# A free place between the first exponentials of one head group, in a two-layer graph network kernel

## The chip, the cores and the metric

The kernel runs on one core of one Trainium2 chip. The metric is the device time of one execution in microseconds; the time of a kernel is the median over its runs. Five engines work in parallel[...]: TensorE (PE, with its weight loads shown as PEld), VectorE (DVE), ScalarE (ACT), GpSimd (POOL) and SyncE (SP), which here only issues transfers.

## The reference

Input `x` holds 128 graphs of 64 nodes with 768 features, `adj` a 64 x 64 adjacency for each graph. Two layers follow each other, both with a residual and a layer norm:

```python
# layer 0: similarity attention, three linear maps of h
u = einsum('bld,bmd->blm', h, h) / sqrt(d)
delta = softmax(u) * adjacency
attn = delta / (delta.sum(2) + 1e-10)
ctx = attn_left @ (h W_left + b) + diag(attn) * (h W_self + b) + attn_right @ (h W_right + b)
x = layernorm(x + relu(layernorm(ctx) * gamma + beta))
# layer 1: 12 heads of 64, masked softmax attention within each graph
q, k, v = split_heads(x @ Wq + bq), split_heads(x @ Wk + bk), split_heads(x @ Wv + bv)
scores = where(adj > 0, q k^T / sqrt(64) + 0.1 * adj, -9e15)
x = layernorm(x + softmax(scores) @ v)
```

Everything is fp32.

## The kernel before

The 8192 tokens are cut into 16 blocks (`NBLK`) of 512 tokens (eight graphs, four tiles of 128). The main loop runs over the blocks `n`. One pass of it interleaves the first layer of block `n + 1` with the second layer of block `n`, in this order on PE: the left and right products of block `n + 1` (`both_sides`, a nested seven-product scheme, from the fourth block on; two plain `side_part` calls before), its self product (`self_part`), the values of block `n` (`values`), and then the queries and keys of block `n` in three stages (`projected`, for head groups `hg` 0, 1 and 2, of four heads each). The last pass has no first layer; it begins with PE transposes (`transposed1`) and does the values last.

Each large product is done by a Strassen-like scheme of seven smaller products in place of eight. `seven` runs over them in the order `ORDER = (1, 2, 6, 5, 7, 4, 3)`, and for each over `j` = 0, 1. In `projected`, `j` = 0 is the queries and `j` = 1 the keys. That gives 14 places in a stage, each with three matmuls of 256 columns. Products 1, 6, 7 and 4 of one `j` accumulate one after the other on one PSUM bank (`ps_X`), products 2, and then 5 and 3, on another (`ps_Y`). Between them the partial sums are read out. This reading out is called eviction here. In `projected`, ACT evicts products 1, 6 and 7 to `uqk` with the bias (L801) and product 4 to `q` or `k` (L807); DVE adds `uqk` to products 2, 5 + 7 and 3 (L809). A matmul that accumulates on a bank can only run when the eviction of what the bank held is done: 4 needs the eviction of 7, and 7 that of 6. In `both_sides` (`nested`, `sub`) the inner products have the same dependences, with the order 6, 5, 7, then 1 and 2 of the next outer product, then 4 and 3; ACT's share of their evictions is the copy at L441.

Attention of a head group is done behind its projection. `scores(n, hg)` for head group 0 is called at place 2 of the stage of head group 1, for head group 1 at place 2 of the stage of head group 2, and for head group 2 in the next pass. It runs the 64 small score matmuls (L833), scales them on DVE (L837), and puts the rest into the queue `urgent`, as items: add the mask (L860), reduce to the maximum (L861), subtract it (L862), four steps of exponentials, a gap, and two transpositions on DVE (turn 0 and turn 1, L857). One step of exponentials is four ACT instructions of 32 rows by 256 elements (L853) and belongs to 32 partitions. `weighted` later multiplies with the values (L882), and its DVE evictions with the division (L892) go into the queue `first`.

After each place, `step` takes at most one item from each of three queues, `first`, `urgent` and `lazy`, in that order. The kind of an item says whether it may go now. An item of DVE work (no kind) goes only when no other such item has gone in this step. An `act` item goes only when ACT is free by plan: `seven`, called by `projected`, forbids it after two places. A `gap` goes always, and fills its place with nothing. In `sub`, `step` takes only from `first` and `urgent` behind inner products 5, 1 and 4, and no DVE item there. `settle` empties a queue up to the named items; `scores` calls it for all attention items that are left. After a first part that sets up the weights, the schedule is manual: on every engine the instructions run in the order in which they were written out.

In block 0 the weights of the first layer are also made ready for the nested scheme (`deepened`): three items at the head of `urgent`, from place 9 on of the head group 2 stage. In the lazy queue are, among others, the last normalizations of the first layer (L720). `finish` ends a block with sums and squares on ACT (L938, L941), a root, and stores.

The line that keeps ACT free after the places of the second half of 5 and the first half of 7:

```python
step(not taps_by_act or (i, j) not in ((5, 1), (7, 0)))
```

Of the kernel before, what the change touches and what calls it, by code (L numbers as in the profile page):

```python
# [17 lines left out]
P = 128  # L18
# [8 lines left out]
Q = 32  # L27
# [24 lines left out]
def gnn_two_layers(ctx: ExitStack, tc, x, adj, wl, bl, ws, bs, wr, br, gamma, beta,  # L52
# [68 lines left out]
    def later(key, *fs, queue=lazy):  # L121
        queue.extend((key, f) if callable(f) else (key, *f) for f in fs)

    def act(f):
        return f, "act"
# [7 lines left out]
    GAP = (gap, "gap")  # L133
# [24 lines left out]
    def freed():  # L158

        while first:  # L160
            first.popleft()[1]()

    def settle(key):

        for queue in (first, urgent, lazy):
            while any(item[0] == key or item[0][0] == key for item in queue):
                queue.popleft()[1]()
# [646 lines left out]
    def scores(n, hg, at_once=1, pool=None, gaps=1):  # L814

        blk = blocks[n]
        q, k = blk["qk"]  # L820
        settle("e")
        settle(("m", n))
        freed()

        s = l1s_p.tile([P, T * 4 * L], F32, tag="s", name="s").rearrange("p (t c r m) -> p t c r m", t=T, c=2, r=2)
        sc = [ps_mm.tile([P, T, 2, L], F32, tag="mm", name=f"sc{r}") for r in range(2)]
        for t in range(T):
            for c in range(2):
                for r in range(2):
                    rows = slice(r * HD, (r + 1) * HD)  # L830
                    for g in range(2):
                        tok = slice(t * P + g * L, t * P + (g + 1) * L)
                        nc.tensor.matmul(sc[r][g * L : (g + 1) * L, t, c, :], lhsT=q[rows, c, tok],  # L833
                                         rhs=k[rows, c, tok], start=True, stop=True)
        m8, add = blk["m8"], blk["add"]
        for r in range(2):
            nc.vector.tensor_tensor(s[:, :, :, r, :], sc[r], m8[:, :, None, :].to_broadcast([P, T, 2, L]), ALU.mult)  # L837
        s4 = s.rearrange("p t c r m -> p t (c r) m")
        s8 = s.rearrange("p t c r m -> p (t c r) m")
        pairs = s.rearrange("p t c r m -> p (t c) (r m)")  # L840
        mx = st.tile([P, T * 4], F32, tag="mx1", name="mx1")

        def exponentials(groups):
            if 0 in groups:
                blk["eT", hg] = (pool or l1e_p).tile([P, T, 2, P], F32, tag="lr" if pool else "eT", name="eT")
            e = blk["eT", hg].rearrange("p t c i -> p (t c) i")
            for a in groups:
                rows = slice(a * Q, (a + 1) * Q)
                for b in range(P // Q):
                    cols = slice(b * Q, (b + 1) * Q)  # L850
                    to = (b, a) if n < NBLK - 1 else (a // 2 * 2 + b % 2, b // 2 * 2 + a % 2)
                    to = [slice(k * Q, (k + 1) * Q) for k in to]
                    nc.scalar.activation(e[to[0], :, to[1]], pairs[rows, :, cols], AF.Exp)  # L853

        def turn(h):
            e = blk["eT", hg][:, h * 2 : h * 2 + 2].rearrange("p t c i -> p (t c i)")
            nc.vector.transpose(e, e)  # L857

        later(("e", n, hg),
              lambda: nc.vector.tensor_tensor(s4, s4, add[:, :, None, :].to_broadcast([P, T, 4, L]), ALU.add),  # L860
              lambda: nc.vector.tensor_reduce(mx, s8, AX.X, ALU.max),  # L861
              lambda: nc.vector.tensor_tensor(s8, s8, mx[:, :, None].to_broadcast([P, T * 4, L]), ALU.subtract),  # L862
              *[act(partial(exponentials, range(a, a + at_once))) for a in range(0, P // Q, at_once)], *[GAP] * gaps,
              *([partial(turn, 0), partial(turn, 1)] if pool is None else [lambda: (turn(0), turn(1))]), queue=urgent)

    def weighted(n, hg):
# [153 lines left out]
    for n in range(NBLK):  # L1020
# [20 lines left out]
        if p >= 0:  # L1041
            one = left if not last else qk[0]
            at(one, 2, scores, p, 2, *((1,) if last else (2, None, 4)))
            at(one, 5, weighted, p, 1)
            if not last and m < DEEP:
                at(left, 13, weighted, p, 2)
                at(right, 0, finish, p)
            elif not last:
                at(right, 1, weighted, p, 2)
                at(right, 2, finish, p)  # L1050
            else:
                at(qk[1], 5, weighted, p, 2)
# [84 lines left out]
        else:  # L1137
            transposed1(n)
            at(qk[0], 9, lambda: later(("m", n), *mask(n), queue=urgent))
            blocks[n]["S"] = combined(blocks[n]["xT"])  # L1140
            combined4(blocks[n]["S"])
        at(qk[1], 2, scores, n, 0)
        at(qk[2], 2, scores, n, 1)
        if not last:
            at(qk[2], 5, weighted, n, 0)
# [136 lines left out]
```

## Time and profile before

| What | us |
|---|---|
| Median of 3 runs (2923.8 to 2925.47) | 2923.98 |
| The profiled execution's own time | 2923.8 |
| Its span in the trace | 2922.1 |
| PE busy (98% of the span) | 2872.4 |
| PE weight loads busy (66%) | 1931.7 |
| DVE busy (68%) | 1979.6 |
| ACT busy (38%) | 1120.4 |
| POOL busy (25%) | 732.2 |
| ACT exponentials, L853, 768 of 414 ns | 317.8 |
| ACT evictions of queries and keys, L801, 288 of 471 to 473 ns | 136.0 |
| PE waits for these evictions (16 times) | 9.5 |

Lines such as L801 are lines of the kernel. A row of a timeline gives the start in us from the span's start, the duration, the engine, the line, the operation with output and input tiles and shapes, the number of instructions merged into the row, and in brackets how long the engine sat idle before and what released it. One fp32 matmul appears as two records, so that a place of a projection stage, three matmuls, has six. Matmuls are pipelined: one starts before the end that is shown for the one before it, and that end is modelled. The granted clock of TensorE was 0.998 of full speed.

### The profile page before, as it was taken

The page shows a single profiled execution, that of the slowest core. Times are in us where ns is not written, and L with a number is a line of the kernel's source. Part 1 is how long each engine was busy: PE and PEld are TensorE (multiplying, and loading weights), DVE is VectorE, ACT ScalarE, POOL GpSimd, SP SyncE. Part 2 cuts the span into 40 slices and gives each one's busy share as a digit, 9 for nine tenths or more (in the row PEclk, how much of TensorE's full clock was granted, in tenths as well). Part 3 has the DMA queues.
Part 4 walks back from the last instruction along what each step waited for, and adds up shares of the span by engine and source line. Part 5 has one row for each costly group of instructions (what it writes and reads, how often), then busy time and mean ns, then how long its engine had stood idle before and what let it go on. Part 6 is the DMA issues. An engine that isn't in the chain of part 4 may idle for free.

```text
span 2922.1 us, 49871 instructions
## 1 busy us (share of the span) xinstructions
PE 2872.4 (98%) x17578; PEld 1931.7 (66%) x17578; DVE 1979.6 (68%) x3973; ACT 1120.4 (38%) x2107; POOL 732.2 (25%) x879
## 2 busy tenths in 40 slices
PE   9999999999999999999999999999999999999997
PEld 5658566585665857657576675766757567585685
DVE  6778777676676766757667576766767667676655
ACT  0005224354243443434444334343434424354255
POOL 3133123213042140412405123051230512314110
PEclk9999999999999999999999999999999999999999
DMA  9788877859577595875958669486694956849443
GB/s 340 231 272 272 251 214 202 243 143 286 153 207 238 160 274 149 226 220 167 270 145 246 195 181 267 137 269 174 184 260 138 285 160 195 246 139 288 140 127 100
DMA packets 440662, 613.18 MB, mean 210 GB/s; under 512 B 53584, under 2 KB 416720, under 8 KB 440416
## 3 DMA queue, kind: packets, MB, share of 16 engines
q1 hardware_dynamic: 362960, 495.93, 56.5%
q10 hardware_dynamic: 60848, 44.05, 8.0%
q0 software_dynamic: 16608, 70.01, 6.6%
q8 instruction: 143, 2.34, 0.3%
q14 instruction: 103, 0.84, 0.1%
HBM read 539.43 MB, written 77.27 MB: 211 GB/s over the span
## 4 chain that ended last, share of the span: by engine, by line
PE 93%; ACT 3%; POOL 2%; DVE 1%; issue 1%; DMA 0%; POOLq 0%; SPq 0%; ACTq 0%
PE ps_X L389 36%; PE ps_Y L389 27%; PE ps_Y L643 11%; PE ps_X L643 10%; PE ps_ctx L682 3%; ACT eT L853 2%; PE sc L833 2%; PE ps_y L882 2%; PE u L532 2%; POOL q L342 1%; ACT L853 1%; ACT uqk L801 1%; PE ps_x L291 0%; POOL q L341 0%; POOL q L343 0%
## 5 line engine op out<-in xcount | busy, mean ns | idle before, releaser
L389 PE MATMUL ps_X<-xT,wqk 128*128 128x256 f32 x1728 | 395.8, 381 | 9.5 <-ACT uqk L801 9.5
L853 ACT ACTIVATE eT<-s 32x256 f32<-32x256 f32 x768 | 317.8, 414 | 172.4 <-DVE s L862 162.4
L389 PEld LDWEIGHTS ps_X<-xT,wqk 128*128 128x128 f32 x1728 | 325.8, 190 | 67.0 <-ACT uqk L801 16.2
L322 POOL TENSOR_TENSOR S<-hT 128x768 f32<-128x768 f32 x16 | 28.9, 1807 | 1132.7 <-PE ps_Y L389 1102.1
L389 PE MATMUL ps_Y<-S,wqk 128*128 128x256 f32 x1152 | 264.3, 379 | 0.0
L687 ACT ACTIVATE unused<-o 128x768 f32<-128x768 f32 x60 | 50.6, 844 | 499.6 <-DVE o L684 346.1
L389 PEld LDWEIGHTS ps_Y<-S,wqk 128*128 128x128 f32 x1152 | 218.9, 190 | 29.8
L443 DVE TENSOR_TENSOR lr<-ps_Y,u_deep 128x384 f32<-128x384 f32 x273 | 152.1, 557 | 109.1 <-PE ps_Y L643 83.4
L643 PE MATMUL ps_Y<-wlr,q 128*128 128x384 f32 x546 | 208.5, 491 | 0.0
L389 PE MATMUL ps_X<-wv,xT 128*128 128x384 f32 x576 | 195.5, 489 | 0.0
L801 ACT ACTIVATE uqk<-ps_X,bq 128x256 f32<-128x256 f32 x144 | 68.1, 473 | 325.0 <-PE ps_X L389 323.9
L809 DVE TENSOR_TENSOR q<-ps_Y,uqk 128x256 f32<-128x256 f32 x144 | 61.0, 424 | 177.5 <-ACT uqk L801 89.3
L389 PE MATMUL ps_X<-ws,hT 128*128 128x384 f32 x540 | 179.2, 486 | 0.0
L643 PE MATMUL ps_X<-wlr,q 128*128 128x384 f32 x364 | 151.0, 497 | 14.6 <-POOL q L342 6.0
L389 PEld LDWEIGHTS ps_X<-wv,xT 128*128 128x128 f32 x576 | 108.0, 190 | 80.4 <-issue 8.4
L892 DVE SCALAR_TENSOR_TENSOR o<-ps_y,rz,o 128x64 f32<-128x64 f32 x720 | 154.7, 278 | 6.4
L443 DVE TENSOR_TENSOR u_deep<-ps_X,lr 128x384 f32<-128x384 f32 x195 | 107.5, 551 | 68.2 <-PE ps_X L643 66.6
L389 PEld LDWEIGHTS ps_X<-ws,hT 128*128 128x128 f32 x540 | 102.5, 190 | 71.4
L643 PEld LDWEIGHTS ps_Y<-wlr,q 128*128 128x128 f32 x546 | 101.6, 190 | 67.2
L420 DVE TENSOR_TENSOR u<-ps_X,bv 128x384 f32<-128x384 f32 x96 | 53.4, 557 | 132.5 <-PE ps_X L389 132.5
L389 PE MATMUL ps_X<-S,wqk 128*128 128x256 f32 x576 | 138.2, 385 | 0.0
L389 PE MATMUL ps_Y<-xT,wqk 128*128 128x256 f32 x576 | 135.6, 385 | 0.0
(258 smaller groups left out, 5471.6 us busy)
## 6 DMA issues: line engine op xcount, KB each, us to landing
wlr<-lr_d SPq DMA_DIRECT2D x819, 192.0 KB, 3.5
wqk<-qk_d SPq DMA_DIRECT2D x672, 192.0 KB, 2.4
wv<-d_v SPq DMA_DIRECT2D x192, 192.0 KB, 2.7
ws<-d_s SPq DMA_DIRECT2D x180, 192.0 KB, 5.8
wv<-in_L_gnn_Wv_dram SPq DMA_DIRECT2D x144, 192.0 KB, 4.1
ws<-in_L_gnn_W_self_dram SPq DMA_DIRECT2D x135, 192.0 KB, 5.4
xa<-in_x_dram SPq DMA_DIRECT2D x64, 384.0 KB, 5.3
sq<-in_x_dram ACTq DMA_DIRECT2D x56, 384.0 KB, 7.7
```

Source lines behind the costliest of these rows:

```text
L389: nc.tensor.matmul(ps, lhsT=a, rhs=b, start=(c == 0 and i in (1, 2, 5)), stop=(c == len(fs) - 1), skip_group_check=True)
L420: recent["u"] = evicted[nm] = nc.vector.tensor_tensor(u, ps, bias[nm][:, b * HALF : (b + 1) * HALF], ALU.add)
L443: nc.vector.tensor_tensor(dst, view(ps), add, ALU.add)
L532: nc.tensor.matmul(u[g * L : (g + 1) * L, t, :], lhsT=xT[:, c, tok], rhs=xT[:, c, tok], start=(c == 0), stop=(c == KC - 1))
L643: nc.tensor.matmul(ps, lhsT=a, rhs=b, start=(k == 0 and j in (1, 2, 5)), stop=(k == len(fs) - 1), skip_group_check=True)
L682: nc.tensor.matmul(ps[g * L : (g + 1) * L, 0:HALF], lhsT=blk["aT"][:, t, g * L : (g + 1) * L], rhs=blk["lr"][t][:, g, cols], start=True, s ...
L801: nc.scalar.activation(u, ps, AF.Identity, bias=bias["qk"[j]][:, c : c + 1])
L809: nc.vector.tensor_tensor(dst, ps, part, ALU.add)
L833: nc.tensor.matmul(sc[r][g * L : (g + 1) * L, t, c, :], lhsT=q[rows, c, tok], rhs=k[rows, c, tok], start=True, stop=True)
L853: nc.scalar.activation(e[to[0], :, to[1]], pairs[rows, :, cols], AF.Exp)
L882: nc.tensor.matmul(y[r, h][cols, t, c, :], lhsT=eT[rows, 2 * h + t, c, cols], rhs=v[rows, 2 * h + t, g, hg + c * HC, :], start=True, stop= ...
L892: nc.vector.scalar_tensor_tensor(res[:, r, c, hg, :], ps[:, t, c, 0:HD], rz[:, t, c : c + 1], res[:, r, c, hg, :], ALU.mult, ALU.add)
```

## The change

The list of items that `scores` puts into `urgent` gets one `GAP` more, for head group 1 alone (`hg == 1`) and in all 16 blocks: behind the first of the four steps of exponentials. The other head groups keep their list. Nothing else is edited.

```diff
               lambda: nc.vector.tensor_reduce(mx, s8, AX.X, ALU.max),
               lambda: nc.vector.tensor_tensor(s8, s8, mx[:, :, None].to_broadcast([P, T * 4, L]), ALU.subtract),
-              *[act(partial(exponentials, range(a, a + at_once))) for a in range(0, P // Q, at_once)], *[GAP] * gaps,
+              *(part for a in range(0, P // Q, at_once) for part in
+                (act(partial(exponentials, range(a, a + at_once))), *([GAP] if hg == 1 and a == 0 else []))),
+              *[GAP] * gaps,
               *([partial(turn, 0), partial(turn, 1)] if pool is None else [lambda: (turn(0), turn(1))]), queue=urgent)
```

## The prediction

> **What bounds the kernel now.** I began with the page's busy times and its chain that ended last, since they say which engine sets the end.
>
> ```profile
> PE 2872.4 (98%) x17578; PEld 1931.7 (66%) x17578; DVE 1979.6 (68%) x3973; ACT 1120.4 (38%) x2107; POOL 732.2 (25%) x879
> ...
> PE 93%; ACT 3%; POOL 2%; DVE 1%; issue 1%; DMA 0%; POOLq 0%; SPq 0%; ACTq 0%
> ```
>
> TensorE (PE) carries 93% of the chain. From one projection stage to the same one a block later it takes 179.75 us, over and over. So a change is worth the time by which it moves PE's starts, and nothing else. The list of waits, PE's alone, says where PE stands for ScalarE (ACT):
>
> ```profile
> PE ps_X L389 <- ACT uqk L801: 9.5, 16, 0.6
> ```
>
> Sixteen waits of 0.59 us. I went through PE's timeline for all 16. Fifteen lie at one place, in the projection of head group 2 in blocks 0 to 14 (284.44, 468.38, 648.13, ... 2802.55 us). The sixteenth, at 2780.98, is in head group 1 of block 14. Block 15 has none. This is ACT's timeline, then PE's, in block 4 (start, duration, engine, line, operation, idle before):
>
> ```profile
> 1001.87 0.47 ACT L801 ACTIVATE uqk<-ps_X,bk 128x256 f32<-128x256 f32 x1 [2.11 <-PE ps_X L389]
> 1002.36 1.28 ACT L853 ACT_TABLE_LOAD   x1
> 1003.66 3.40 ACT L853 ACTIVATE eT<-s 32x256 f32<-32x256 f32 x8
> 1007.08 0.47 ACT L801 ACTIVATE uqk<-ps_X,bq 128x256 f32<-128x256 f32 x1
> 1007.46 0.47 ACT L801 ACTIVATE uqk<-ps_X,bk 128x256 f32<-128x256 f32 x1
> 1007.95 1.69 ACT L853 ACTIVATE eT<-s 32x256 f32<-32x256 f32 x4
> 1009.66 0.47 ACT L807 ACTIVATE q<-ps_X,bq 128x256 f32<-128x256 f32 x1
> 1010.16 1.69 ACT L853 ACTIVATE eT<-s 32x256 f32<-32x256 f32 x4
> 1011.87 0.47 ACT L807 ACTIVATE k<-ps_X,bk 128x256 f32<-128x256 f32 x1
> 1013.74 0.48 ACT L441 COPY u_deep<-ps_X 128x384 f32<-128x384 f32 x1 [1.39 <-PE ps_X L643]
> ```
>
> ```profile
> 983.34 5.34 PE L389 MATMUL ps_X<-xT,wqk 128*128 128x256 f32 x24
> 988.52 2.75 PE L389 MATMUL ps_Y<-S,wqk 128*128 128x256 f32 x12
> ...
> 1004.26 2.75 PE L389 MATMUL ps_X<-xT,wqk 128*128 128x256 f32 x12
> 1007.61 2.86 PE L389 MATMUL ps_X<-xT,wqk 128*128 128x256 f32 x12 [0.59 <-ACT uqk L801]
> 1010.30 2.75 PE L389 MATMUL ps_Y<-S,wqk 128*128 128x256 f32 x12
> 1012.89 0.81 PE L643 MATMUL ps_X<-wlr,hT 128*128 128x384 f32 x2
> 1013.54 1.45 PE L643 MATMUL ps_Y<-wlr,hT 128*128 128x384 f32 x4
> 1014.83 0.81 PE L643 MATMUL ps_X<-wlr,q 128*128 128x384 f32 x2
> ```
>
> I write (7,0) for product 7 of the queries, (7,1) of the keys. (7,·) starts at 1004.26, (4,·) at 1007.61, (3,·) at 1010.30. The eight exponentials in one piece (3.40 us) are the first two steps; the eviction of (7,0) stands behind them until 1007.08, and (4,0), which accumulates on the same bank, waits for it. One stage earlier (first two lines) the same two products run without a stop: 988.52 - 983.34 = 5.18 us. Here they take 1010.30 - 1004.26 = 6.04. **The wait therefore costs 0.86 us**, more than the 0.59 shown, because modelled ends overlap the next start[...].
>
> [...] (7,0) was ready at about 1005.82 and was evicted at 1007.08. [...] so I reckon in starts. [...] here the load is 1.28 us and the exponential follows after 0.02[...]. [...] in the trace they lead by 0.2 to 0.3 us, but at 1007.61 weight load and matmul start together, so the wait holds both.
>
> **The change part by part.** No instruction is added or removed. One empty item enters the queue behind step 0 of the exponentials. Step 0 still leaves behind (6,1). The item uses up the place behind (5,0), where step 1 went. Behind (5,1) and (7,0) no ACT item may go, so step 1 follows the eviction of (7,1), step 2 that of (4,0), step 3 that of (4,1); the gap falls behind (3,0), the first transposition (turn 0, L857) behind (3,1), turn 1 into the next stage, behind its (7,2), since behind its first product no VectorE (DVE) item is taken.
>
> *Saved.* Step 0 ends at 1003.66 + 1.69 = 1005.35. In a stage that isn't held, evictions start 1.56 and 2.85 us after (7,·) starts (block 15: products at 2864.10, evictions at 2865.66 and 2866.95). So (7,0) is evicted 1005.82 to 1006.29 and (7,1) 1007.11 to 1007.58, both before (4,0) at 1006.85 and (4,1) at 1008.15 need them. Saved: 0.86.
>
> *Given back.* ACT now idles 0.47 us before the first eviction and 0.82 before the second, and pays it at the end. With the spacings of the trace (eviction to exponentials 0.49 to 0.50, exponentials to what follows 1.71): step 1 at 1007.60, (4,0) evicted at 1009.31, step 2 at 1009.81, (4,1) at 1011.52, step 3 at 1012.02, ended at 1013.71, the next stage's copy L441 from 1013.73 to 1014.21. Nothing else queues on ACT there. That copy drains product (7,1) of the nested left/right products, and their (7,6), now at 1014.83, accumulates on its bank. Moved up by 0.86, (7,6) would start at 1013.97. The copy lets it start at 1014.21 + 0.06 (as from 1007.55 to 1007.61) = 1014.27: 0.30 late, plus 0.07 for the refill (after the POOL wait at 1034.61 the next start is 0.72 later, otherwise 0.65). Given back: 0.37. **Net 0.49 per block.**
>
> *Covered by other work.* Turn 0 heads DVE's queue until step 3 ends (1013.71) and runs 0.70 to about 1014.45; behind it the L443 eviction then ends near 1015.0, turn 1 near 1015.7. The next score multiply needs products that end near 1016.2, and nobody needs the turned tile before 1022.02. So 0; without that 0.5 us of cover, DVE's delay would pass to the scores. The DVE evictions of (7,·) come earlier. GpSimd (POOL) runs its sums from 1004.51 to 1017.1 whatever PE does, then has slack:
>
> ```profile
> 1024.76 0.45 POOL L341 TENSOR_TENSOR q<-hT 128x128 f32<-128x128 f32 x1 [7.64 <-PE ps_Y L643]
> ```
>
> The later 0.2 to 0.5 us waits of PE for POOL are released through PE itself and move with it. SP's weight loads are unmoved in order and wait for buffers that PE frees; PE waits for no load in these stages. No DMA issue is moved past anything; the four stores of the first layer (POOL, L725, at 1014.96) keep their place.
>
> *Blocks that differ.* Blocks 1 to 13 are as above: 13 × 0.49 = 6.4. Block 0 is followed by a plain side product whose first eviction is on DVE: the whole 0.86. Two subtraction steps on weights and their stores also take three places there, so that the gap stands where turn 0 stood; one normalization (L720, 0.68 us) moves from 314.36 to about 294, ahead of the two waits for L857 at 318.82 and 320.70 (0.76 and 1.18). I estimate 0.5 of these goes; bounds 0 and 1.2. Sum 1.3. Block 14 is followed by 24 PE transposes with eight ACT copies (2808.41 to 2811.71). Step 3 ends at about 2808.6, the copies near 2811.94, 0.23 later than now; POOL's three sums after them end 0.23 later too, at about 2817.49, and product 6 needs them (now they end at 2817.26 and it starts at 2817.51). It loses the 0.86 and about 0.3 more: -0.3, bounds -0.6 and 0.86. Block 15 has no table load and no wait; the items it pushes later (the summing L938 from 2871.74 to 2873.55) are needed at 2880.77 only: 0.
>
> Sum: 6.4 + 1.3 - 0.3 = 7.4 us. The profiled execution took 2923.8 with a span of 2922.1; span after 2914.7, execution 2916.4, and 0.2 more for the median (2923.98): **2916.6 us**.
>
> **The rivals.** All turn on C, the end of that copy: a block gives back C - 1013.84.
>
> - *No new wait* (C under 1013.9): 13 × 0.86 + 1.0 = 12.2, 2911.8. For it: the copy's product ends at 1012.9 already. Against: 1.29 us of new idle time on ACT.
> - *The wait only moves* (C near 1014.7): gain about 1, 2923. For it: the margin is thin; a block must give back under 0.49 for the total to pass 0.2% (5.85 us), so C under 1014.33, only 0.12 above my figure. Against: each spacing is read in the same stage.
> - *Slower*: the same ACT chain, stretched. Beyond C = 1015.23 a block loses 0.53 and the total 5.9. It would take another 1.0 us in the three steps (each exponential 0.50 instead of 0.41), or a fourth step behind the copy. At C = 1015.5: 13 × -0.80 + 1.0 = -9.4, 2933.4. Against: the exponentials span only 398 to 418 ns over all 768.
> - *The edit does nothing*: the place would have to be taken behind (5,1). The existing trace has step 2 behind (7,1), so ACT places are counted as I do. Time 2924; I give it 2 in 100.
>
> **How the numbers follow.** The forecast 0.68 (its own range 2914 to 2920), no new wait 0.05, wait only moved 0.17, nothing 0.02, slower 0.08. About 0.2% is what a measurement of this kernel can tell from no change. Of the 0.68 I put 0.58 beyond it and 0.10 within, because 5.85 lies inside its range: faster 0.58 + 0.05 = 0.63, same 0.10 + 0.17 + 0.02 = 0.29, slower 0.08. The range leaves out the slower case and most of the first rival: 2912.5 to 2923.
>
> **What would show it.** In each of blocks 0 to 14: four exponentials, two evictions of uqk, four exponentials, one eviction, four, one, four; no wait of PE for uqk in head group 2 (one left in all, in block 14); in its place 13 waits of PE on ps_X L643 for ACT u_deep L441 of about 0.3 us; period 179.25 instead of 179.75. I am wrong if those 13 waits are absent or over 0.8, if PE's POOL waits grow, or if the scores of the next stage start later after (7,6) than 0.8 us.

## The result and the profile after

The changed kernel takes 2917.45 us (median of 10 runs, 2915.97 to 2918.6) against 2924.51 for the kernel before in the same comparison. The ratio is 0.9975 with a 95% interval of 0.9966 to 0.9983, so 7.1 us faster. Forecast were 2916.6 us and 7.4 us.

The page's chain that ended last, and three lines of PE's list of waits (time in total, times, longest), of the kernel after:

```profile
PE 96%; POOL 2%; issue 1%; DVE 1%; ACT 0%; DMA 0%; POOLq 0%; SPq 0%; ACTq 0%
```

```profile
PE ps_X L643 <- issue: 5.6, 29, 0.2
...
PE ps_X L643 <- POOL q L343: 2.1, 10, 0.2
...
PE ps_X L389 <- ACT uqk L801: 0.6, 1, 0.6
```

ACT's 3% of the chain are gone. Of sixteen waits for the evictions of queries and keys one is left, at 2775.15 us in head group 1 of block 14, which the edit doesn't touch. ACT's timeline in block 4, and then PE's, as shown of before:

```profile
1002.35 1.70 ACT L853 ACTIVATE eT<-s 32x256 f32<-32x256 f32 x4
1004.51 0.47 ACT L801 ACTIVATE uqk<-ps_X,bq 128x256 f32<-128x256 f32 x1 [0.46 <-PE ps_X L389]
1005.81 0.47 ACT L801 ACTIVATE uqk<-ps_X,bk 128x256 f32<-128x256 f32 x1 [0.82 <-PE ps_X L389]
1006.30 1.70 ACT L853 ACTIVATE eT<-s 32x256 f32<-32x256 f32 x4
1008.03 0.47 ACT L807 ACTIVATE q<-ps_X,bq 128x256 f32<-128x256 f32 x1
1008.53 1.69 ACT L853 ACTIVATE eT<-s 32x256 f32<-32x256 f32 x4
1010.23 0.47 ACT L807 ACTIVATE k<-ps_X,bk 128x256 f32<-128x256 f32 x1
1010.72 1.69 ACT L853 ACTIVATE eT<-s 32x256 f32<-32x256 f32 x4
1012.42 0.48 ACT L441 COPY u_deep<-ps_X 128x384 f32<-128x384 f32 x1
```

```profile
1002.96 5.34 PE L389 MATMUL ps_X<-xT,wqk 128*128 128x256 f32 x24
1008.13 2.75 PE L389 MATMUL ps_Y<-S,wqk 128*128 128x256 f32 x12
1010.73 0.81 PE L643 MATMUL ps_X<-wlr,hT 128*128 128x384 f32 x2
1011.37 1.45 PE L643 MATMUL ps_Y<-wlr,hT 128*128 128x384 f32 x4
1013.00 0.88 PE L643 MATMUL ps_X<-wlr,q 128*128 128x384 f32 x2 [0.18 <-issue]
1013.82 1.16 PE L833 MATMUL sc<-k,q 64*64 64x64 f32 x64
```

Both evictions now start when their product ends, with ACT idle 0.46 and 0.82 us ahead of them. Products 7 and 4 run through in 1008.13 - 1002.96 = 5.17 us (6.04 before). The price stands at the end: the copy L441 has no idle time before it any more (1.39 before) and ends at 1012.90, and (7,6) starts at 1013.00, where 1011.37 + 1.29 = 1012.66 was possible (1.29 us is the same step before, from 1013.54 to 1014.83). So it starts 0.34 late.

The spans differ by 5.8 us only (2922.1 and 2916.3). The profiled execution of after lost 1.5 us at its start, where PE's waits for the first input sum to 7.1 us instead of 5.6: the scores in block 0's head group 2 stage start at 272.34 instead of 270.83. From there to the first product of the last values it is 2601.04 us before (270.83 to 2871.87) and 2593.72 after: 7.3 us, which agrees with the medians. Below I use this part of each trace, called the stretch, beside the medians.

### The profile page after: what moved, and what is told of

Read it like the earlier page. It is cut to its first block, busy times and chain, and to the rows that moved or that the text cites. A ratio compares the mean times of both kernels' runs of the same rounds, so it can differ in the third digit from the quotient of the medians.

```text
span 2916.3 us, 49872 instructions
## 1 busy us (share of the span) xinstructions
PE 2872.5 (98%) x17578; PEld 1932.9 (66%) x17578; DVE 1974.3 (68%) x3973; ACT 1122.4 (38%) x2107; POOL 732.4 (25%) x879
## 4 chain that ended last, share of the span: by engine, by line
PE 96%; POOL 2%; issue 1%; DVE 1%; ACT 0%; DMA 0%; POOLq 0%; SPq 0%; ACTq 0%
PE ps_X L389 38%; PE ps_Y L389 28%; PE ps_Y L643 11%; PE ps_X L643 10%; PE ps_ctx L682 3%; PE sc L833 2%; PE ps_y L884 2%; PE u L532 2%; POOL q L342 1%; POOL q L341 0%; PE ps_x L291 0%; POOL q L343 0%; ACT eT L853 0%; DMA xa<-in_x_dram 0%; DVE u_deep L443 0%
## 5 line engine op out<-in xcount | busy, mean ns | idle before, releaser
L853 ACT ACTIVATE eT<-s 32x256 f32<-32x256 f32 x768 | 317.8, 414 | 171.6 <-DVE s L862 161.6
L643 PE MATMUL ps_Y<-wlr,q 128*128 128x384 f32 x546 | 208.5, 491 | 0.0
L801 ACT ACTIVATE uqk<-ps_X,bq 128x256 f32<-128x256 f32 x144 | 68.3, 474 | 333.1 <-PE ps_X L389 332.4
L643 PE MATMUL ps_X<-wlr,q 128*128 128x384 f32 x364 | 152.0, 499 | 16.8 <-POOL q L342 5.9
L643 PEld LDWEIGHTS ps_Y<-wlr,q 128*128 128x128 f32 x546 | 101.6, 190 | 67.2
```

Of the source, the lines that this page charges most:

```text
L643: nc.tensor.matmul(ps, lhsT=a, rhs=b, start=(k == 0 and j in (1, 2, 5)), stop=(k == len(fs) - 1), skip_group_check=True)
L801: nc.scalar.activation(u, ps, AF.Identity, bias=bias["qk"[j]][:, c : c + 1])
```

## The experiments

My theory: PE waited because the table load and two steps of exponentials stand ahead of the eviction of (7,0); the gap removes that wait, 0.86 us a block, and gives half of it back, because ACT now idles before the evictions and the copy in the next stage comes late. The rivals: the exponentials alone make the wait, with or without the table load; and what is given back comes from something other than that copy, since the profile put the new wait to no engine ("issue").

Each median below stands beside runs of the kernel before in the same comparison: 2924.76 us for the first four experiments, 2924.34 for the last.

**The table load moved, without the gap.** A tiny exponential into a scratch tile loads the table (1.28 us) at a place where ACT is idle for 4.70 us in block 4 of the kernel before:

```diff
+    warm = const.tile([P, 2], F32, tag="warm", name="warm")
+    nc.vector.memset(warm, 0.0)
...
+        def preload():
+            nc.scalar.activation(warm[:, 1:2], warm[:, 0:1], AF.Exp)
+        if not last:
+            if n == NBLK - 2:
+                at(qk[1], 2, preload)
+            at(qk[2], 2, preload)
```

> The kernel before, without the gap; one tiny exponential (128 x 1) ahead of the score matmuls of the head group 2 stage in blocks 0 to 14, and of the head group 1 stage in block 14. It pulls the load of the exponential table (1.28 us) to a place where ACT is idle for 4.70 us. Theory (the wait for uqk is the table load ahead of two exponential steps): steps 0 and 1 then run 1002.36 to 1005.76 in block 4's times of before, the eviction of (7,0) starts at 1005.82 unheld, and the end of the ACT chain isn't moved, so nothing is given back: no PE wait for uqk, none for the L441 copy, 16 x 0.86 = 13.8 us less than before, near 2910.7. Rival (two exponential steps alone hold the eviction): the waits stay, 2924 to 2925.

Measured: 2910.99 us, ratio 0.9957 (0.9943 to 0.9970); the stretch 2587.44, 13.6 less than before. No PE wait for `uqk` is in the list at all. ACT's timeline of this kernel in block 4 (the edit adds two lines ahead, so L853 is L855 here, L801 is L803, and so on):

```profile
991.73 1.28 ACT L1146 ACT_TABLE_LOAD   x1
993.03 0.20 ACT L1146 ACTIVATE warm<-warm 128x1 f32<-128x1 f32 x1
...
999.37 3.38 ACT L855 ACTIVATE eT<-s 32x256 f32<-32x256 f32 x8
1002.94 0.47 ACT L803 ACTIVATE uqk<-ps_X,bq 128x256 f32<-128x256 f32 x1 [0.19 <-PE ps_X L391]
```

The same eight exponentials stand in one piece ahead of the same eviction, and it is ACT that waits for PE, 0.19 us. So two steps alone hold nobody up, and the first rival falls. The load with one step behind it holds nobody up either: in the changed kernel ACT waits 0.46 us for PE behind them. It takes both together: the load of 1.28 us and two steps.

**The table load moved, with the gap.** The same edit in the changed kernel leaves the gap alone to be measured, where there is nothing for it to remove.

> The same tiny exponential in the changed kernel, so the gap stays while the wait that it was to remove is gone by other means. Theory (the gap gives back 0.43 us in each of blocks 1 to 13, because ACT idles ahead of the evictions and the copy L441 comes late): the wait ahead of (7,6) stays as in the changed kernel, 13 x 0.43 = 5.6 us more than the kernel with the tiny exponential alone, about 2916.5. Rival (the gap itself is free, and the wait at (7,6) has another source, such as the earlier start of PE): as the kernel with the tiny exponential alone, 2910.7.

Measured: 2916.62 us, ratio 0.9974 (0.9964 to 0.9984); the stretch 2593.03, so the gap costs 5.6 us here. PE's timeline in block 4, where (7,·) starts at 1002.45 (L643 is L645 here, L833 is L835):

```profile
1012.50 0.88 PE L645 MATMUL ps_X<-wlr,q 128*128 128x384 f32 x2 [0.18 <-issue]
1013.31 1.16 PE L835 MATMUL sc<-k,q 64*64 64x64 f32 x64
```

The time from (7,·) to the next stage's scores is 10.86 us in this kernel, as in the changed one, and 10.44 in the kernel with the moved load and without the gap. **The gap by itself costs 0.42 us a block** in blocks 1 to 13. At the two ends it does something else: block 0 is 0.61 us shorter with it, and block 14 is 0.84 longer. These two nearly offset each other, so the total comes out close to 13 x 0.42.

**Four gaps.** The dose is raised: ACT idles longer ahead of step 1.

```diff
-*([GAP] if hg == 1 and a == 0 else [])
+*([GAP] * 4 if hg == 1 and a == 0 else [])
```

> Four gaps in place of one behind step 0: they use up the places behind (5,0), (5,1), (7,0) and (7,1), so step 1 follows the eviction of (4,0), steps 2 and 3 that of (4,1). Theory (a block gives back the time from 1013.84 to the end C of the copy, in block 4's times of before, plus the 0.05 measured): step 1 at 1008.90, eviction of (4,1) at 1010.61, steps 2 and 3 from 1011.10 to 1014.50, C = 1015.00, given back 1.2, net -0.35 a block; with 1.4 won in block 0 and 0.8 lost in block 14 about 4 us slower than before, 2928.5, and a wait of about 1.1 us ahead of (7,6). Rival (that wait comes from a weight load, from POOL or from the matmul queue, not from ACT's chain): it stays at about 0.2, 2917.5 as the changed kernel.

Measured: 2927.52 us, ratio 1.0009 (1.0003 to 1.0016); the stretch 2603.80, 2.8 more than before. ACT's, PE's and POOL's timeline of this kernel in block 4, where (7,·) starts at 1004.85:

```profile
1015.03 0.48 ACT L441 COPY u_deep<-ps_X 128x384 f32<-128x384 f32 x1
```

```profile
1015.61 0.88 PE L643 MATMUL ps_X<-wlr,q 128*128 128x384 f32 x2 [0.90 <-POOL S L328]
```

```profile
1013.70 1.80 POOL L328 TENSOR_TENSOR S<-S,hT 128x768 f32<-128x768 f32 x1
```

Here the list names POOL's sum, which ends at 1015.50. In the kernel after, the same sum is:

```profile
1011.81 1.82 POOL L328 TENSOR_TENSOR S<-S,hT 128x768 f32<-128x768 f32 x1
```

It ends at 1013.63 there, 0.63 after (7,6) has started, so (7,6) doesn't need it; that the ends fall together in four gaps is chance. The copy ends 0.10 before (7,6) in both kernels (1012.90 and 1013.00, 1015.51 and 1015.61), and with the table load moved and the gap kept again (1012.40 and 1012.50). A block gave back 11.57 - 10.44 = 1.13 us, against 1.2 expected, and the kernel is 2.8 us slower than before, where about 4 were expected from the copy's end.

**Step 3 behind the copy.** The gap stays. Step 3 is held back and put behind the next stage's first eviction. The turns, which stand behind step 3 in the queue, move back with it.

```diff
-*([GAP] if hg == 1 and a == 0 else [])
+*([GAP] * {0: 1, 2: 3}.get(a, 0) if hg == 1 else [])
...
-*[GAP] * gaps,
+*[GAP] * (0 if hg == 1 else gaps),
...
+                at(left, 1, last_step)    # last_step, left out here, issues items up to step 3
```

> The gap behind step 0 stays; step 3 is held back by three gaps behind step 2 and then put, in the next stage, behind the eviction of its first product, so the copy L441 runs ahead of step 3; the turns follow it without a gap. Theory (the copy is late only because step 3 stands ahead of it): the copy ends near 1013.4 in block 4's times of before, no wait ahead of (7,6), the whole 0.86 in blocks 1 to 14 and 1.4 in block 0: 13.4 us less than before, near 2911.1. Rival (the turns on DVE or step 3's result, which both come later here, are what the next stage waits for): no better than the changed kernel, 2917 to 2922.

Measured: 2912.34 us, ratio 0.9960 (0.9948 to 0.9973); the stretch 2588.50, 12.5 less than before. ACT's timeline and PE's in block 4:

```profile
1010.86 0.48 ACT L441 COPY u_deep<-ps_X 128x384 f32<-128x384 f32 x1 [0.86 <-PE ps_X L643]
1011.36 1.69 ACT L853 ACTIVATE eT<-s 32x256 f32<-32x256 f32 x4
```

```profile
1011.95 0.81 PE L643 MATMUL ps_X<-wlr,q 128*128 128x384 f32 x2
```

The copy ends at 1011.34 and (7,6) has no wait, although step 3 now ends at 1013.05 and both turns start later (1013.09): (7,6) needs neither. POOL's sum L328 ends at 1012.91 here, after (7,6) has started, and the edit moves no weight load. From (7,·) to the scores it is 10.44. So what (7,6) waited for was the copy behind step 3. The kernel is about 1 us short of the expectation. In block 0 the wait of 0.76 us for a turn is still there, which is absent in the changed kernel, and that makes 0.61; block 14 wins 0.38 us and not 0.86.

**The gap in block 0 alone, with the table load moved.** This asks where block 0's share comes from, and joins what helps.

```diff
-*([GAP] if hg == 1 and a == 0 else [])
+*([GAP] if hg == 1 and a == 0 and n == 0 else [])
```

The lines that move the load, shown above, are added too.

> The tiny exponential that loads the table early, and the gap behind step 0 in block 0 alone. Theory (in block 0 the gap won 0.6 us beside the 0.86, because it moves one normalization ahead of the transpositions in the queue, and gives nothing back because a plain side product follows): against the kernel with the tiny exponential alone the wait of 0.76 us for L857 near 318 is gone, the second one stays near 1.2, no wait ahead of (7,6) in blocks 1 to 13, about 0.6 us less, near 2910.4, which a time can't tell from 2910.99 and the trace can. Rival (the 0.6 us came from the freed PE in block 0 and not from the normalization): the wait of 0.76 us stays, 2911.

Measured: 2910.18 us, ratio 0.9950 (0.9936 to 0.9963); the stretch 2586.91, 0.5 less than with the moved load alone and 14.1 less than before. PE's timeline where the third head group of block 0 is multiplied with the values, with the moved load alone, and then with the gap in block 0 (L884 and L886 are L882 of before):

```profile
318.54 0.70 PE L884 MATMUL ps_y<-v,eT 64*64 64x65 f32 x32 [0.76 <-DVE eT L859]
```

```profile
317.82 0.70 PE L886 MATMUL ps_y<-v,eT 64*64 64x65 f32 x32
```

The last normalization starts at 294.72 instead of 314.09, and the wait of 0.76 is gone. PE was freed in both, so the rival that this follows from the freed PE falls. This kernel has the lowest median of all that ran. The times alone can't tell it from the moved load alone (0.9936 to 0.9963 and 0.9943 to 0.9970 overlap); the trace shows the 0.61 us in block 0.

## Why the prediction was right

*Where the bound lies, and the size of the wait.* PE, busy for 98% of the span, sets the time by its starts. The wait was worth 0.86 us a block, not the 0.59 of the list: 6.04 us became 5.17. Of the 0.27 between them 0.16 is the overlap of the modelled end (983.34 + 5.34 = 988.68, and the next start is 988.52), and 0.11 is in the products behind the wait, which took 2.86 us instead of 2.75. A refill as the cause of such a loss, of these 0.11 and of the forecast's 0.07, was my estimate; the trace shows the times alone. Weight loads, too, were held: the first of product 4 came after 1.00 us of idle time and started with its matmul at 1007.61, where the one for 1004.26 had started at 1004.05, 0.21 ahead. With the load moved and nothing given back, the period is 178.88 us instead of 179.75, so 0.87.

*Given back.* Forecast 0.37, measured 0.42. (7,6) was to start 10.01 us after (7,·) and does so after 10.04. The term that was a little short is the delay between the copy's end and the matmul: 0.06 taken, 0.10 measured. What I expected to read there was wrong, and by the letter all three signs of being wrong came about. The list has no wait for ACT `u_deep`; PE's waits for POOL rose from 9.3 us to 11.1; and the scores start 0.81 us after (7,6). None of them touches the mechanism. The 13 waits are there, one in each of blocks 1 to 13, with 0.18 us put to "issue". Nine older waits changed their label from "issue" to POOL L343 (1 before, 10 after), so that "issue" rose by four only, from 25 to 29, and POOL's waits seemed to grow. And 0.81 is the usual 0.74 plus the 0.07 that I had put down to a refill (0.72 us to the next start behind a wait, otherwise 0.65).

*Net in blocks 1 to 13.* Forecast 0.49, measured 0.45 (the period, from 654.42 to 833.71, is 179.29 instead of 179.75), or 5.9 us instead of 6.4.

*Block 0.* Forecast 1.3. From the scores of head group 1 to product 2 of the right part it took 56.40 us (270.83 to 327.23) and takes 54.93: 1.47. With the moved load alone it is 55.54, so the eviction's wait makes 0.86 and the normalization 0.61, where 0.5 was my estimate. The normalization is what takes away the first wait for a turn, as argued; the second is 1.22 after 1.18.

*Block 14.* Forecast -0.3, measured 0.0 (72.67 us from (7,·) to the first product of the last values, and 72.68). As said, the 0.86 doesn't last. Of it 0.72 goes at the transposes, where PE waits for one of ACT's copies:

```profile
2803.36 1.88 PE L291 MATMUL ps_x<-ident,o 128*128 128x128 f32 x12 [0.46 <-ACT xT L292]
```

The rest goes at product 6. The further 0.3 that I took off didn't come, and here a step failed: I read the 0.25 us from the end of POOL's last sum (2817.26) to product 6 (2817.51) as a lag. Before, product 6 waited for nothing: it started 2.70 us after product 2 (2814.81), as it does where nothing holds it (2.69 in block 0, from 271.93 to 274.62). After, the sum ended at 2811.53 and product 6 started at 2811.59, only 0.04 later than 2.70 behind product 2. The copies, too, ended 0.09 later behind (7,·) and not 0.23 (12.60 us, before 12.51).

*The sum.* The parts measured make 5.85 + 1.47 - 0.01 = 7.3 us, as the stretch does; forecast were 7.4. Blocks 1 to 13 gave 0.5 less than forecast, block 0 gave 0.2 more and block 14 0.3 more. That these errors cancel is luck: the parts were known to some tenths, not the total to one.

*Cover.* The turns cost nothing: they run at 1012.43 and 1013.51, and the score multiply starts at 1015.01, when its matmuls are done. POOL's slack fell from 7.64 to 7.28 us, and PE's waits for POOL L342 are 5.9 us after 6.0. One reading was off without effect: POOL's sums end at 1015.00 before, and what runs on to 1017.1 is the issue of the four stores.

*The rivals.* That the wait only moves was half true: half of it moved. No new wait and slower didn't come about in this kernel. The experiments show what each takes: step 3 behind the copy gives the first, four gaps the second.

## What to carry to other kernels

Look for long work that stands ahead of an eviction which TensorE waits for. Held back here, it left ACT idle for 0.46 and 0.82 us ahead of two evictions, and the copy behind the last step came so late that (7,6) started 0.34 us late. So ask who needs the first item behind that work, and when, before you count the gain: here 0.87 us a block was saved and 0.42 given back. Look first for what made the queue long: here one table load on top of two steps. A tiny activation pulled it into an idle stretch, with no cost to be seen in these traces, and that was worth 13.6 us where the better order was worth 7.3.

## What the runs showed of the hardware

In block 4 of the kernel before, ACT took nothing ahead of the two steps of exponentials: the eviction of (7,0), ready at about 1005.82, started at 1007.08, when they had ended at 1007.06.

A tiny exponential (128 x 1, 0.20 us) was enough to place the table load (1.28 us at 991.73); the exponentials that follow 6 us later, at 999.37, start without one. The profile's name for a wait was not its cause: the same wait for a copy is "issue" (0.18 us) in the kernel after and a POOL sum (0.90 us) with four gaps. What told the cause was a lag of 0.10 us behind the copy's end in three kernels.

DVE's busy time fell from 1979.6 to 1974.3 us with the same 3973 instructions. The normalizations L720 account for it, with 45.8 us after 51.7: three of them in a row in block 4 take 2.13 us after and 2.59 before. They run at the same time as some of POOL's sums, and those change too: in block 4 POOL's L344 takes 0.77 us before, beside L720, and 0.45 after, clear of it, while L343 takes 0.73 before and 1.04 after. Why both change, no run here shows.
